# GpSimd's queue put under the kernel's own clock in a two-layer graph kernel

## The chip, the cores and the metric

The kernel runs as one program on one core of one Trainium2 chip. The metric is the device time of that core in microseconds, the median of three runs. The engines are named as the profile names them: PE (TensorE, with PEld for its weight loads), DVE (VectorE), ACT (ScalarE), POOL (GpSimd) and SP (SyncE, which here only issues transfers).

## The reference

Input is `x`, 64 batches of 256 x 256 in float32, and one adjacency `adj` of 256 x 256. Two layers follow each other, each with a layer norm and a ReLU ahead and a residual sum behind:

```python
# layer 0: three products with (adj * adj), two ReLUs between them
h = jnp.maximum(_layernorm(x, axis=-1), 0.0)
x = x + _L0_gnn_ref(h, adj, adj, L0_gnn_W1, L0_gnn_W2, L0_gnn_W3)
# layer 1: needs the eigenvectors U of the normalised Laplacian of adj
h = jnp.maximum(_layernorm(x, axis=-1), 0.0)
x = x + _L1_gnn_ref(h, adj, L1_gnn_W1, L1_gnn_b1, L1_gnn_W2, L1_gnn_b2)
#   _L1: _, U = jnp.linalg.eigh(L_norm); agg = U^T h; h = relu(agg W1 + b1); U (h W2 + b2)
```

Layer 0 does not need U. Layer 1 does, from its first product with U on.

## The kernel before

Two kinds of work run side by side on one core.

**The chain.** Class `Eigen` computes U step by step, mostly on DVE with operands of a few hundred columns: `laplacian`, `tridiagonalize` (254 Householder steps), `leaves` (32 QL steps on small blocks), and `level` four times (blocks of 32, 64, 128 and 256 are merged). PE serves it with small transposes and products into the banks `psA` to `psD`, ACT with squares and copies, POOL with column operations: powers (`power`, a `pow`), copies and masks.

**The layers.** Class `Layers` takes the 64 batches as 32 pairs. `products` is the stream of PE and ACT work of layer 0 (banks `bank`), `rows` the stream of norms. POOL has two kinds of work from them. A norm has three steps on POOL after eight reductions on ACT: `v` (scale and epsilon), `scale` (a `pow` on four columns), `shift`; ACT's ReLU waits for `shift`. And from pair 1 on each pair has three accumulating transfers issued from POOL's queue: `forms<-forms` in `spread_by_seven` and `s<-s` and `s<-forms` in `add`; products behind them wait for their landing.

**The order.** Class `Pace` sees every operation of the chain as it is written (`chain`) and keeps a clock of its own: for each engine the time up to which it is planned, for each tile when it was written and read. Before a chain operation is issued, `run(limit, engine)` issues what the streams have that can start before the chain's operation is due. `due` is when the operation's inputs are ready by that clock, plus 0.4 us for PE and 0.1 us for ACT; whether its engine is free by then isn't part of it. `fits` decides for one stream operation: for PE and ACT its whole length can count, for every other engine it needs only to start before the limit. `issue` advances the clock; for DVE and POOL it lets the clock lag behind an operation by up to `WINDOW` = 1.0 us.

This written order is binding only for the engines that `manual_schedule` names. Around the chain these are PE and ACT. The order of DVE, POOL and SP is left to the framework's scheduler, which lists the instructions anew by its own estimates. In layer 1 (`layer1`, with the last stream) all engines keep the written order. The conditional block `mend`, which is not taken, stands between them.

**A step of the tridiagonalisation, on POOL.** In the first 127 steps (`lo < P`) the written order of POOL's operations is, with the tiles' names of the profile: copy of `alpha` (`m<-xr`), masked column (`xc<-xc,lower`), `power(s0, ...)` (`s<-nn,half`), sign (`q<-xr`), and in the next turn of the loop `none` twice, `gg`, `gu`. DVE's `nb` (`m<-q,s`) needs `s` and `q`; `ac` needs `nb`; `den` needs `nb` and both `none`; `gam` (`z<-den`) needs `den`. The lines from the loop, which are shown shortened, give the order in which they are written:

```python
self.stt(nb, q, 2.0, s0, OP.mult, OP.mult)
self.stt(ac[:, hs], rc[:, hs], nb, xa[:, hs], OP.mult, OP.add)
pu, pr = as_row("psB", ac, halves), as_row("psA", rc, halves)   # PE transposes
nc.gpsimd.tensor_scalar(none, tail, 1e-30, 1e30, OP.is_le, OP.mult)
nc.gpsimd.tensor_tensor(none, none, nn, OP.add)
...
self.stt(den, alpha, nb, none, OP.mult, OP.add)
self.recip(gam, den)
...
aside(lo).tensor_tensor(gg, gam, gam, OP.mult)
```

In the other 127 steps POOL has only the copy, a memset of one column of `xc`, and both `none`. In `leaves` it has one copy a step (`zn`), in each `level` six powers of `rdq`, one of `zh` and one of `rn`.

Of the kernel before, what the change touches and what calls it, by code (L numbers as in the profile page):

```python
# [159 lines left out]
class Pace:  # L160
# [56 lines left out]
        return self.issue(op, self.slower)  # L217

    def fits(self, op, start, limit, engine):
        if engine is None or op.engine not in ("PE", "ACT"):  # L220
            return start < limit
        if engine == "PE":
            return start < limit + self.HOP * (op.engine == "ACT")
        return start + op.busy + self.lead * (op.engine == "ACT") < limit
# [2107 lines left out]
@with_exitstack  # L2332
def tile_kernel(ctx: ExitStack, tc: tile.TileContext, ap):
    pool = ctx.enter_context(tc.tile_pool(name="shared", bufs=1))
    gt2, u, ut = (pool.tile([P, H, N], F32, name=c) for c in ("gt2", "u", "ut"))
    layers = Layers(tc, ctx, ap, gt2, u, ut)
    layers.open(ctx)
    pace = Pace(tc.nc)
    with ExitStack() as inner:
        eigen = Eigen(tc, inner, ap, gt2, pace)  # L2340

        layers.nc = pace.later
        for op in layers.load(0):
            pace.chain(op)
        layers.nc = pace.now
        eigen.load_matrices(1, 2)
        layers.load_weights()
        eigen.load_rest()

        layers.nc, layers.now = pace.later, pace.now  # L2350
        pace.streams = layers.streams()
        with tc.manual_schedule(engines={mybir.EngineType.PE, mybir.EngineType.Activation}):
            eigen.vectors(u, ut)
            pace.go_on(FLAG_US)
        pace.on = False
        eigen.mend(u, ut)
    pace.on, pace.no_haste, pace.slower = True, True, 1.0
    layers.open1(ctx)
    layers.layer1(pace)
# [33 lines left out]
```

## Time and profile before

| | |
|---|---|
| time, median of 3 runs | 2365.49 us (2364.38 to 2368.03) |
| profiled execution | 2369.36 us, span 2367.6 us |
| mean granted clock of PE | 0.994 |
| PE busy, by stage: 0 to 40 us (start) | 22.79 of 40 us |
| 40 to 752 us (tridiagonalisation, first half) | 697.18 of 712 us |
| 752 to 1300 us (second half) | 538.67 of 548 us |
| 1300 to 1686 us (leaves) | 375.02 of 386 us |
| 1686 to 2178 us (levels) | 474.99 of 492 us |
| 2178 us to the end (layer 1) | 181.52 of 189.6 us |
| DVE busy in the five stages from 40 us on | 664.89, 520.75, 355.87, 368.04, 68.66 us |
| POOL busy in the same | 352.48, 151.30, 39.11, 62.16, 81.10 us |

Nearly every instruction is recorded by one helper line (208, the call in `Pace.issue`), so the profile's groups are told apart by tiles, not by lines. An entry "A <- B: 12.9, 32, 1.9" of the waits means that A sat idle 12.9 us in total in 32 places until B came, 1.9 us at the longest. In timeline rows the first number is the start, the second the duration, and the square bracket the idle time of the engine before it with what ended that.

### The profile page before, as it was taken

To read this page: it belongs to the slowest core of one execution; us is meant where nothing else is said; L and a number is where in the kernel's file an instruction comes from. 1 tells how busy PE (TensorE), PEld (TensorE's weight loads), DVE (VectorE), ACT (ScalarE), POOL (GpSimd) and SP (SyncE) were. 2 spreads that over 40 slices of the span, in tenths; PEclk is the share of its full clock that TensorE was granted. 3 is DMA by queue.
4 is the path that set the end of the run, shared out by engine and by line. 5 is a ranking of instruction groups with operands and counts; after the bars stand their busy time and mean duration, and the time that the engine had idled before them with its cause. 6 is when DMAs were issued, how large, how long until landed. Compare 5 with 4: busy or idle time off the path is not lost. (4 is left out here: it accounts for less than half of the span.)

```text
span 2367.6 us, 40804 instructions
## 1 busy us (share of the span) xinstructions
PE 2290.2 (97%) x10652; PEld 1854.7 (78%) x10652; DVE 2005.0 (85%) x12072; ACT 1183.8 (50%) x2951; POOL 698.7 (30%) x1946
## 2 busy tenths in 40 slices
PE   7999999999999999999999899999999999999999
PEld 4687878787777877787888788777778777887888
DVE  7999999999999999999999899999877687882343
ACT  4455554555555555555555345555554455543322
POOL 3444544445554222222222001111111111111443
PEclk9999999999999999999999999999999999999999
DMA  4022222122222222222222222322322222223675
GB/s 134 23 70 61 65 57 70 51 69 63 59 59 62 72 56 61 69 67 59 72 63 60 58 63 72 72 72 59 72 63 63 59 58 72 54 63 103 217 251 203
DMA packets 91359, 183.26 MB, mean 77 GB/s; under 512 B 8432, under 2 KB 61808, under 8 KB 91120
## 3 DMA queue, kind: packets, MB, share of 16 engines
q0 software_dynamic: 13392, 73.14, 15.6%
q1 hardware_dynamic: 77728, 107.45, 13.4%
q8 instruction: 86, 1.41, 0.2%
q14 instruction: 153, 1.25, 0.2%
HBM read 65.48 MB, written 41.94 MB: 45 GB/s over the span
## 5 line engine op out<-in xcount | busy, mean ns | idle before, releaser
L208 PE MATMUL bank<-forms,L_gnn_W 128*128 128x256 f32 (+2 forms) x2102 | 490.7, 382 | 9.2 <-DVE x L208 6.1
L208 PE MATMUL bank<-L_gnn_W,s 128*128 128x256 f32 x2086 | 476.0, 378 | 4.8 <-ACT s L208 4.7
L208 PEld LDWEIGHTS bank<-forms,L_gnn_W 128*128 128x128 f32 x2102 | 390.6, 191 | 73.3 <-issue 11.7
L208 PEld LDWEIGHTS bank<-L_gnn_W,s 128*128 128x128 f32 x2086 | 391.7, 192 | 57.3 <-ACT s L208 5.7
L208 ACT ACTIVATE s<-bank 128x512 f32<-128x512 f32 (+1 forms) x485 | 278.7, 579 | 174.3 <-PE bank L208 173.3
L208 PE MATMUL bank<-forms,sums 128*128 128x256 f32 (+1 forms) x1512 | 347.0, 377 | 0.0
L208 PEld LDWEIGHTS bank<-forms,sums 128*128 128x128 f32 x1512 | 283.3, 191 | 53.4 <-issue 15.5
L208 PE MATMUL bank<-gt,s 128*128 128x256 f32 (+1 forms) x1036 | 246.3, 377 | 1.1 <-ACT s L208 1.1
L208 PE MATMUL bank<-L_gnn_W,y 128*128 128x512 f32 (+3 forms) x538 | 230.8, 572 | 1.1 <-ACT y L208 1.1
L208 ACT ACTIVATE forms<-bank 128x512 f32<-128x512 f32 x217 | 128.9, 594 | 180.9 <-PE bank L208 180.7
L208 PEld LDWEIGHTS bank<-gt,s 128*128 128x128 f32 x1036 | 188.9, 190 | 24.8 <-ACT s L208 2.6
L208 POOL COPY m<-xr 128x1 f32<-128x1 f32 x254 | 59.9, 236 | 418.1 <-DVE xr L208 418.0
L208 PEld LDWEIGHTS bank<-L_gnn_W,y 128*128 128x128 f32 x538 | 98.7, 190 | 98.2 <-issue 87.3
L208 ACT ACTIVATE junk<-xr 128x254 f32<-128x254 f32 (+63 forms) x127 | 46.0, 362 | 200.5 <-DVE xr L208 200.4
L208 ACT ACTIVATE junk<-x 128x256 f32<-128x256 f32 x256 | 105.8, 413 | 71.9 <-issue 44.0
L208 DVE SCALAR_TENSOR_TENSOR A<-xr,wc,A 128x255 f32<-128x255 f32 (+63 forms) x381 | 139.2, 368 | 0.0
L208 DVE SCALAR_TENSOR_TENSOR A<-wr,q,A 128x255 f32<-128x255 f32 (+63 forms) x381 | 138.0, 365 | 0.0
L208 ACT ACTIVATE junk<-x,nm 128x256 f32<-128x256 f32 x256 | 128.7, 503 | 4.0
L208 PE MATMUL bank<-p,gt 128*128 128x512 f32 (+2 forms) x272 | 122.8, 567 | 0.0
L208 PE MATMUL bank<-gt,h 128*128 128x256 f32 (+1 forms) x520 | 119.1, 379 | 0.1
L208 DVE SCALAR_TENSOR_TENSOR r<-A,xr 128x255 f32<-128x255 f32 (+63 forms) x381 | 117.8, 309 | 0.2
L208 PE MATMUL psB<-ident,ac 128*128 128x128 f32 x381 | 84.7, 277 | 27.2 <-DVE z L208 15.0
(614 smaller groups left out, 4639.5 us busy)
## 6 DMA issues: line engine op xcount, KB each, us to landing
x<-in_x_dram SPq DMA_DIRECT2D x128, 256.0 KB, 3.0
x<-x SPq DMA_DIRECT2D x64, 512.0 KB, 3.5
forms<-forms POOLq DMA_DIRECT2D x31, 768.0 KB, 5.8
s<-s POOLq DMA_DIRECT2D x31, 768.0 KB, 5.9
s<-forms POOLq DMA_DIRECT2D x31, 768.0 KB, 5.8
hw<-hw SPq DMA_DIRECT2D x64, 256.0 KB, 3.1
out_dram<-out SPq DMA_DIRECT2D x64, 256.0 KB, 2.2
L_gnn_W<-in_L_gnn_W_dram SPq DMA_DIRECT2D x1, 2048.0 KB, 11.2
```

What stands on the lines that cost most here:

```text
L208: return op.call(*op.args, **op.kwargs)
```

## The change

POOL joins the engines whose written order is binding around the chain, and `fits` gets a rule for it: when the chain's next operation is one of POOL, a stream's operation for POOL goes ahead of it only if it would also end before the chain's is due. When the chain's next operation is one of another engine, a POOL operation of the streams still needs only to start before the limit. The order on PE and ACT stays written by the same clock, that of DVE and SP stays with the framework's scheduler. No instruction is added or taken away.

```diff
     def fits(self, op, start, limit, engine):
+        if engine == "POOL" == op.engine:
+            return start + op.busy < limit
         if engine is None or op.engine not in ("PE", "ACT"):
             return start < limit
...
-        with tc.manual_schedule(engines={mybir.EngineType.PE, mybir.EngineType.Activation}):
+        with tc.manual_schedule(engines={mybir.EngineType.PE, mybir.EngineType.Activation, mybir.EngineType.Pool}):
             eigen.vectors(u, ut)
             pace.go_on(FLAG_US)
```

## The prediction

> **What bounds the kernel now.** The busy times of the page come first.
>
> ```profile
> PE 2290.2 (97%) x10652; PEld 1854.7 (78%) x10652; DVE 2005.0 (85%) x12072; ACT 1183.8 (50%) x2951; POOL 698.7 (30%) x1946
> ```
>
> PE has 2290.2 us of work in a span of 2367.6 us. The change adds no work for it, so the time can only move by PE's idle time, now 77.4 us: 17.2 us before 40 us, 14.8 and 9.3 in the two halves of the tridiagonalisation, 11.0 in the leaves, 17.0 in the levels, 8.1 in layer 1 (from the busy times by stage). Second, the list of waits, all engines, for who holds PE and DVE up:
>
> ```profile
> DVE m L208 <- PE psB L208: 40.7, 4, 13.1
> ...
> DVE r L208 <- PE psB L208: 22.6, 75, 1.0
> ...
> PE psB L208 <- DVE z L208: 15.0, 19, 1.9
> DVE m L208 <- POOL s L208: 12.9, 32, 1.9
> ```
>
> The first row is the levels: the chain there waits for PE in four places, up to 13.1 us, so a POOL step that holds the chain up by a few us costs nothing. The second and third are the tridiagonalisation: in 75 steps the chain waits for PE, in 19 PE for the chain. There the two run neck and neck and a late chain costs PE time. The last is POOL's part: 32 times `nb` (m) waited for the power. Third, POOL's timeline in a usual step (its copy at 158.78 is left out) and in one of five steps that had the written order already:
>
> ```profile
> 158.93 0.51 POOL L208 TENSOR_SCALAR q<-xr 128x1 f32<-128x1 f32 x1
> 159.41 0.20 POOL L208 TENSOR_TENSOR xc<-xc,lower 128x2 f32<-128x2 f32 x1
> 159.70 0.32 POOL L208 TENSOR_SCALAR none<-m 128x1 f32<-128x1 f32 x1
> 160.10 0.61 POOL L208 TENSOR_TENSOR s<-nn,half 128x1 f32<-128x1 f32 x1
> 160.69 0.35 POOL L208 TENSOR_TENSOR none<-none,nn 128x1 f32<-128x1 f32 x1
> ```
>
> ```profile
> 472.74 0.29 POOL L208 TENSOR_TENSOR xc<-xc,lower 128x2 f32<-128x2 f32 x1
> 473.25 0.66 POOL L208 TENSOR_TENSOR s<-nn,half 128x1 f32<-128x1 f32 x1 [0.23 <-DVE nn L208]
> 473.91 0.26 POOL L208 TENSOR_SCALAR q<-xr 128x1 f32<-128x1 f32 x1
> 474.25 0.26 POOL L208 TENSOR_SCALAR none<-m 128x1 f32<-128x1 f32 x1
> 474.59 0.24 POOL L208 TENSOR_TENSOR none<-none,nn 128x1 f32<-128x1 f32 x1
> ```
>
> Now q and the first `none` go ahead of the power s; then s goes first and q and both `none` come behind it. Fourth, the largest idle stretch of PE in the levels: POOL's timeline, PE's, and the windows' row (columns: stretch, length, busy PE, PEld, DVE, ACT, POOL, granted clock, DMA share, GB/s).
>
> ```profile
> 1764.14 0.72 POOL L208 TENSOR_TENSOR rdq<-rdq,half 128x2 f32<-128x2 f32 x1 [4.36 <-DVE rdq L208]
> 1764.94 0.19 POOL L208 TENSOR_SCALAR v<-v 128x4 f32<-128x4 f32 x1
> 1765.22 1.01 POOL L208 TENSOR_TENSOR scale<-v,rsqrt 128x4 f32<-128x4 f32 x1
> 1766.30 0.20 POOL L208 TENSOR_TENSOR shift<-nm,scale 128x4 f32<-128x4 f32 x1
> ```
>
> ```profile
> 1769.61 2.93 PE L208 MATMUL bank<-L_gnn_W,s 128*128 128x256 f32 x6 [3.76 <-ACT s L208]
> ```
>
> ```profile
> 1768.50:1772.70 4.20, 3.09 (x7) 2.52 (x8) 0.18 (x1) 4.20 (x8) 0.00 (x0) 0.50 0.54 186
> ```
>
> A norm's steps stood behind the chain's power, which waited for DVE. ACT's last reduction for `v` ended at 1762.25. PE then sat 3.76 us and ran 4.2 us at half clock, 2.1 us more.
>
> **The change part by part.** All is set against the profiled span (2367.6 us; that execution took 2369.36) and carried to the median of 2365.49 as a difference.
>
> *1. Levels: the norm no longer stands behind the chain's power.* The chain is ahead of PE there (40.7 us of waits), so by the planner's clock, which goes with PE, the norm's steps come first. From 1762.3 they need 0.19 + 1.01 + 0.20 and some 0.15 of gaps, to 1763.85, before the power's input (DVE's rdq, ending 1763.98). ACT is free at 1763.89, so its ReLU, which started at 1766.54, comes 2.65 us earlier; 1.1 us of the gap stay. A gap of 2.47 us at 1326 kept full clock, so the half clock goes too: -2.65 - 2.1 = -4.7 us. Bounds: 0 (order unchanged) and -5.9. In the leaves and levels the other steps (zn, zh, rn, 0.2 to 0.7 us each) may now queue behind a norm or a transfer (0.97 us to issue); the cover is the 40.7 us, which if gone would make each such wait cost its 1 us.
>
> *2. First half: the power goes ahead.* Of the 12.9 us, six waits are followed at once by an idle PE (23.36, 492.71, 537.94, 559.37, 630.00, 678.78: 1.62, 0.95, 0.42, 0.96, 1.43, 0.66, in all 6.0 us). The `none` ahead of s takes about 0.32 to 0.40 us from its start to that of s (159.70 to 160.10); norms pushed ahead of the copy make up the rest. So between 6 x 0.32 = 1.9 and 6.0 us; I take -3.5, near the middle, as part of the norms stay in front.
>
> *3. First half: both `none` come later.* In the five steps of written order `den` waited 0.07, 0.07, 0.17, 0.02 and 0.13 us, 0.092 on average, so 127 x 0.092 = 11.7 us on the chain. PE pays only where it had no other work: in 48 of the 127 steps the transposes began within 0.2 us of the end of `ac`. 48 x 0.092 = +4.4 us. In one of the five (583 us) DVE had `ac` ahead of `den`; if the scheduler did that everywhere, PE's transposes would come 0.13 us earlier, -2.3 us in the 18 recorded waits; with queued durations at their means `none` is 0.16 us late, +7.7. Bounds -2.3 and +7.7.
>
> The row that speaks against this part is the sign step: q takes 223 to 723 ns, 458 in the middle, for one column. [...]
>
> *4. Layer steps ahead of `none`.* This is the price that no row shows. In the program `none` is written behind `ac` and PE's transposes, and before a PE operation the streams may put on POOL whatever starts up to 0.4 us after `ac` is ready; the new rule guards only POOL's own operations. The scheduler had `none` ready before `den` in all but 12 steps. I took the time at which each layer step got its input from ACT, and counted those from 0.35 us before the end of `nn` to 0.46 us after `ac`: 26 of 50 in the first half, 20 of 40 in the second. With 1.0 us for a transfer, 1.25 for a norm's first two steps and 0.6 for the two `none`, `den` is late by 39.4 and 24.6 us, 64 in all, 1.39 a step. Behind it wait z, gc and gr on DVE, and with them the next step's transposes. Of each 1.39 us, 0.82 fit into the median time from `ac` to DVE's read of the transposes, and 0.25 into the mean slack of PE (0.40 less the least, 0.15): 0.32 x 46 = 14.7 us. A third of it I take as planned for already, since the chain's 22.6 us of waits for PE are room that the planner left and the chain didn't use: +10 us. Bounds 0 (all hidden) and 64 - 22.6 = 41.
>
> The rest goes together: the memset of `xc` in the second half now stands between the copy and `none` (0.12 us, beside DVE's work), and the DMAs issued are the same, on the same queue; SP's are not moved.
>
> Sum: -4.7 - 3.5 + 4.4 + 10 = +6.2, so 2371.7 us.
>
> **The rivals.**
>
> *Faster.* The scheduler lists DVE with POOL's new order in view and puts `ac` and the read of the transposes ahead of a late `den`; then parts 3 and 4 cost nothing, and 1 and 2 stay: 2365.5 - 8.2 = 2357.3. For it: the order of 583 us was of that kind. It decides if `den` is late by less than the 0.82 us hole in most of the 46 steps. Against: DVE is busy 664.9 of 712 us there, so displaced work finds little room.
>
> *No change.* Part 4 is half hidden and half planned, +2 in place of 10: 2363.7.
>
> *Much slower.* The chain outgrows its cover. After 2178 us PE has only 58 matmuls of layer 0 left beside layer 1: 42 of 0.215 us, 8 of 0.43, 8 of 0.11, 13.4 us. If half of the 64 us stays on the chain, with 11.7 from part 3 and less 3.5, it is 40 us longer; past 13.4 every us counts: +27 - 4.7 = 2388.
>
> **How the numbers follow.** The forecast gets 0.38, much slower 0.12, no change 0.22, faster 0.28. Three runs of before lie within 0.15%, so about 0.2% (4.7 us) is what can be told from no change. Chances: faster 0.28, same 0.22, slower 0.50. The range reaches from 2355 (the faster case and its bound in part 1) to 2389; the forecast's own is 2364 to 2382.
>
> **What would show it.** Right: the idle time at 1769 falls to about 1 us without a half clock; `m <- POOL s` falls below 5 us; `den <- POOL none`, 3.6 us now, rises above 20; norms and transfers stand between q and `none`; PE's waits for the chain before 1300 us rise from 27 to 35 us or more. Wrong: `den <- POOL none` stays under 10 us, or PE's idle time falls below 70 us.

## The result, and the profile after

| | before | after |
|---|---|---|
| median | 2366.35 us (2364.38 to 2368.03, 4 runs) | 2396.16 us (2394.48 to 2398.02, 4 runs) |
| ratio | | 1.0126, 95% interval 1.0109 to 1.0144 |
| profiled execution | 2369.36 us, span 2367.6 | 2394.48 us, span 2392.7 |
| PE idle, 40 to 752 and 752 to 1300 us | 14.8 and 9.3 us | 32.2 and 21.4 us |

The kernel is 29.8 us slower. The two profiled executions lie 25.1 us apart, since that of before is 3.0 us above its median and that of after 1.7 us below. PE has the same instructions; of the 25.1 us, 22.5 are more idle time of PE (99.9 in place of 77.4 us) and 2.6 more busy time:

```profile
PE 2292.8 (96%) x10652; PEld 1852.9 (77%) x10652; DVE 2011.9 (84%) x12072; ACT 1180.6 (49%) x2951; POOL 688.6 (29%) x1946
```

The list of waits of all engines shows who made PE and DVE idle:

```profile
DVE rb L208 <- POOL rdq L208: 46.5, 24, 6.7
...
DVE den L208 <- POOL none L208: 39.3, 53, 2.3
...
PE psB L208 <- DVE z L208: 29.0, 29, 2.5
...
DVE r L208 <- PE psB L208: 26.5, 57, 2.0
...
PE psB L208 <- DVE xr L208: 23.0, 30, 2.3
```

`den` waits 39.3 us for `none`, where it waited 3.6. The profile puts PE's waits for its transposes down to `z` (29.0 us, before 15.0), which comes from `den`, and to the next row `xr` (23.0, before 10.6). The transposes themselves read `ac`, not `z`; all waits put down to `z` lie in steps in which DVE has `den` ahead of `ac`. Both rows tell that the chain comes late for PE. The first row is the levels' part, and harmless, as will be seen.

PE's order is the same in both kernels, all 10652 matmuls in the same sequence (ACT's too, but for one copy at 43 us). So the start of each matmul after, less its start before, is a lag that can be followed (times are those of before):

| at | 90 us | 302 | 460 | 775 | 1093 | 1357 | 1700 | 1754 | 1932 | 2162 | 2277 |
|---|---|---|---|---|---|---|---|---|---|---|---|
| lag, us | -2.3 | 11.7 | 16.2 | 22.6 | 30.8 | 38.5 | 41.6 | 41.4 | 29.8 | 27.7 | 25.0 |

Up to 1357 us, early in the leaves, the lag grows by 40.8 us, in the rest of the leaves by 3.1; the levels give 13.9 back, layer 1 another 2.7. This last part goes with the clock: behind PE's stops at 2158 and 2194 us, of 4.8 and 2.8 us in both kernels, the half clock lasted 6.8 us each before and 3.4 us each after. The -2.3 us at 90 us are no effect of the change: a kernel whose POOL is left to the scheduler until 1300 us shows -1.8 there, and the profiled execution of before lies 3.0 us above its median.

A bad step, with the second longest wait of all, by POOL's timeline of after and by DVE's:

```profile
195.67 0.36 POOL L208 TENSOR_SCALAR q<-xr 128x1 f32<-128x1 f32 x1
197.30 0.19 POOL L208 TENSOR_SCALAR v<-v 128x4 f32<-128x4 f32 x1 [1.27 <-ACT junk L208]
197.58 1.03 POOL L208 TENSOR_TENSOR scale<-v,rsqrt 128x4 f32<-128x4 f32 x1
198.68 0.24 POOL L208 TENSOR_SCALAR none<-m 128x1 f32<-128x1 f32 x1
199.00 0.19 POOL L208 TENSOR_TENSOR none<-none,nn 128x1 f32<-128x1 f32 x1
```

```profile
196.81 0.22 DVE L208 SCALAR_TENSOR_TENSOR ac<-A,m,xa 128x2 f32<-128x2 f32 x1
...
199.23 0.22 DVE L208 SCALAR_TENSOR_TENSOR den<-m,none 128x1 f32<-128x1 f32 x1 [2.13 <-POOL none L208]
...
200.14 0.38 DVE L208 SCALAR_TENSOR_TENSOR r<-psB,xr 128x229 f32<-128x229 f32 x1
```

After the sign step POOL has the norm's `v` next. Its input isn't there: POOL stands for 1.27 us with both `none` ready behind it, then does `v` and `scale`. `den` waited 2.13 us. DVE had done `ac` before that, and PE began the transposes at 198.16, but their read (`r<-psB`) stands behind `den` on DVE and comes late with it. In 47 places with a layer step ahead of `none`, `den` waited over 0.15 us, 38.2 us in all; up to 21.7 us of this fall into the time in which POOL stood idle for the layer step's input.

How much of the lag that explains: between the ends of successive `nn`, the step lengths of both kernels can be subtracted. 67 of the 249 steps compared have a layer step ahead of the second `none`; they grew by 24.4 us (34 steps, first half) and 17.3 us (33, second half), 41.7 in all. The 182 others changed by +1.1 and -4.3 us.

In the levels, the place that the prediction had chosen, by POOL's timeline, PE's, and the windows' row of after:

```profile
1803.72 0.23 POOL L208 TENSOR_SCALAR v<-v 128x4 f32<-128x4 f32 x1 [4.09 <-ACT junk L208]
1804.04 1.01 POOL L208 TENSOR_TENSOR scale<-v,rsqrt 128x4 f32<-128x4 f32 x1
1805.02 0.69 POOL L208 TENSOR_TENSOR rdq<-rdq,half 128x2 f32<-128x2 f32 x1
1805.68 0.20 POOL L208 TENSOR_TENSOR shift<-nm,scale 128x4 f32<-128x4 f32 x1
```

```profile
1808.99 3.29 PE L208 MATMUL bank<-L_gnn_W,s 128*128 128x256 f32 x14 [1.75 <-ACT s L208]
```

```profile
1808.00:1812.20 4.20, 3.21 (x15) 2.86 (x16) 3.05 (x24) 4.20 (x7) 0.69 (x1) 1.00 0.39 125
```

The norm no longer stands behind the power, though the power slipped in between `scale` and `shift`. PE's stop fell from 3.76 to 1.75 us, and the clock stayed full. And a second stop went that the prediction hadn't touched, here PE's timeline of before and of after at the same matmul:

```profile
1878.49 2.07 PE L208 MATMUL bank<-forms,L_gnn_W 128*128 128x256 f32 x4 [3.61 <-DVE x L208]
```

```profile
1908.33 3.62 PE L208 MATMUL bank<-forms,L_gnn_W 128*128 128x256 f32 x16
```

Before, a layer's addition on DVE (`x<-x,bank`) came late because DVE was deep in the chain's work. The chain's lead explains it, by the waits between 1725 and 2205 us of after:

```profile
DVE m L208 <- PE psB L208: 7.0, 4, 3.5
```

It was 40.7 us. POOL's `rdq` now stands behind layer steps, DVE waits 46.5 us for it in place of 20.7, and so the chain no longer runs ahead of PE. That the addition finds room in these waits is read from the two traces; no run took the one without the other.

### The profile page after: what moved, and what is told of

It reads as the page before. It is cut to its first block, busy times and chain, and to the rows that moved or that the text cites. A ratio compares the mean times of both kernels' runs of the same rounds, so it can differ in the third digit from the quotient of the medians.

```text
span 2392.7 us, 40790 instructions
## 1 busy us (share of the span) xinstructions
PE 2292.8 (96%) x10652; PEld 1852.9 (77%) x10652; DVE 2011.9 (84%) x12072; ACT 1180.6 (49%) x2951; POOL 688.6 (29%) x1946
## 3 DMA queue, kind: packets, MB, share of 16 engines
q1 hardware_dynamic: 77728, 107.45, 13.5%
## 5 line engine op out<-in xcount | busy, mean ns | idle before, releaser
L208 PEld LDWEIGHTS bank<-forms,L_gnn_W 128*128 128x128 f32 x2102 | 390.5, 191 | 69.1 <-issue 11.7
L208 PEld LDWEIGHTS psB<-ident,ac 128*128 128x128 f32 x381 | 45.8, 136 | 116.7 <-issue 61.1
```

What stands on the lines that cost most here:

```text
L208: return op.call(*op.args, **op.kwargs)
```

## The experiments

Each is set against the kernel before on the same chip.

| kernel | median | before | ratio, 95% |
|---|---|---|---|
| `none` first, planner's order redrawn | 2369.54 | 2367.28 | 1.0013 (1.0003 to 1.0022) |
| bound from the leaves on | 2357.72 | 2367.28 | 0.9960 (0.9946 to 0.9974) |
| bound in the tridiagonalisation only | 2404.06 | 2367.28 | 1.0161 (1.0144 to 1.0178) |
| without the rule in `fits` | 2397.84 | 2367.28 | 1.0131 (1.0114 to 1.0148) |
| `none` first, PE's order kept | 2359.69 | 2367.62 | 0.9967 (0.9954 to 0.9979) |
| the same, with a load on POOL | 2413.68 | 2367.62 | 1.0188 (1.0171 to 1.0205) |
| the same, old order of the chain's steps | 2357.08 | 2367.62 | 0.9954 (0.9938 to 0.9971) |
| a wider rule | 2426.01 | 2367.62 | 1.0236 (1.0219 to 1.0254) |
| bound from the levels on | 2353.69 | 2367.03 | 0.9945 (0.9931 to 0.9958) |

**1. `none` first, planner's order redrawn.**

```diff
             nb = nbs[:, k : k + 1]
+            none = self.col("none", 1)
+            nc.gpsimd.tensor_scalar(none, tail, 1e-30, 1e30, OP.is_le, OP.mult)
+            nc.gpsimd.tensor_tensor(none, none, nn, OP.add)
...
             pu, pr = as_row("psB", ac, halves), as_row("psA", rc, halves)
-            (the same three lines)
```

> POOL's order is still written out for the whole kernel; only the two instructions that make `none` are written at the top of the step, ahead of `ac` and of PE's transposes, so that no layer step can be put between q and them. Theory 1 (the time went into layer steps that stand ahead of `none`: 67 steps, 41.7 us, with 13.5 us given back in the levels): about 2350 to 2360 us, and `den <- POOL none` falls from 39.3 us to below 8. Theory 2 (the chain order s, q, none itself is slower, as such): 2385 to 2400 us, with `den <- POOL none` about as now.

2369.54 us. 27 us of the loss went with two instructions that were written some lines earlier, and `den` waits 5.3 us. 22 steps keep a layer step ahead of `none` (it stands ahead of the copy or the sign step there); they grew by 0.03 us in all, so a layer step costs nothing there, and its place is what counts. But the time lies 10 us above theory 1's range, which left out that the planner's clock, which now counts `none` earlier, draws PE's order anew (10688 matmuls in place of 10652, as the planner cuts some in two).

**2, 3. One part of the kernel at a time.** `vectors` is split behind the tridiagonalisation; only the blocks for which POOL is named differ.

```diff
         with tc.manual_schedule(engines={PE, Activation}):
-            eigen.vectors(u, ut)
+            reflections = eigen.vectors(u, ut)      # tridiagonalisation
+        with tc.manual_schedule(engines={PE, Activation, Pool}):
+            eigen.behind(u, ut, reflections)        # leaves, levels
```

> POOL's order is written out from the leaves on only; in the tridiagonalisation the scheduler orders POOL as in the kernel before. Theory 1 (the loss is in the tridiagonalisation, the gain of 13.5 us in the levels is independent of it): 2350 to 2355 us, the stop of PE near 1769 us short and at full clock, PE's idle time before 1300 us as in the kernel before. Theory 2 (the levels give time back only because the tridiagonalisation ran late and left less to catch up): 2362 to 2368 us, no gain.

> POOL's order is written out in the tridiagonalisation only; from the leaves on the scheduler orders POOL. Theory 1 (both parts are independent): 2396 + 13.5 = about 2410 us (2404 to 2412). Theory 2 (the levels' recovery comes with the late start, not with POOL's order): 2393 to 2399 us.

2357.72 and 2404.06 us (in the third kernel Pool is named in the first block and not in the second). Against before on the same chip that is -9.6 and +36.8, together +27.2; the change as a whole brought +29.8. So the two parts are independent to within 2.6 us, and theory 2 falls in both. Run 2 is 3 us above theory 1's range, run 3 at the lower end of its own, 6 us under its number. For run 2 the same lags show why: that kernel loses 5.2 us in the leaves (from -0.6 at 1250 us to +4.6 at 1700), before the levels give 13.5 back. Run 9 takes that up. For run 3, the leaves' loss, which it doesn't have, makes up 4 of the 6 us.

**4. The rule in `fits` left out.**

```diff
-        if engine == "POOL" == op.engine:
-            return start + op.busy < limit
```

> All of the change but the new rule in `fits`: a chain operation of POOL is then fitted into the clock with PE's 0.4 us of grace, like the others. PE's and ACT's order stay the same, POOL's differs in some hundred places. Theory 1 (the rule guards POOL's own operations only, and the loss comes in front of PE's operations, which it doesn't guard): within 0.5% of the change, 2392 to 2408 us, `den <- POOL none` 39 us or somewhat more. Theory 2 (the rule itself is what makes the order bad, by pushing layer steps from q and s to the place behind them): 2365 to 2380 us, `den <- POOL none` well below 39 and `m <- POOL s` back at 10 or more.

2397.84 us, `den` waits 39.1 us for `none`. (PE's 0.4 us of grace, which the expectation names, don't enter for a POOL operation: without the rule a layer's step needs only to start before the chain's is due.) The rule made no difference that can be told: it guards the places in front of POOL's own operations, and the costly ones lie in front of PE's transposes.

**5. `none` first, with PE's order kept.** The planner's clock still counts `none` at its old place; only the instructions are written earlier.

```diff
             nb = nbs[:, k : k + 1]
+            none = ...    # both instructions, written directly, not by the clock
...
-            nc.gpsimd.tensor_scalar(none, ...)
-            nc.gpsimd.tensor_tensor(none, ...)
+            self.planned(...)    # the same two: counted by the clock, not written
```

> As the kernel with `none` at the top of the step, but the planner's clock still counts the two `none` at their old place, so that PE's and ACT's orders stay those of the change, matmul for matmul; only POOL's order differs, with 27 layer steps left ahead of `none` (all of them ahead of the copy or the sign step too) in place of 69. Theory 1 (layer steps ahead of `none` are the whole loss, and the 15 us that the first experiment lacked were PE's redrawn order): 2396.2 - 41.7 = 2354.5 us (2350 to 2359). Theory 2 (those 15 us belong to POOL's written order): 2365 to 2372 us.

2359.69 us, all 10652 matmuls in the order of the change. So 36.5 us of the change's time are the place of `none` behind the layer steps, and 9.9 us of the first experiment's time came with PE's redrawn order. The time lies 0.7 us above theory 1's range and 5.2 above its number; `den` still waits 7.5 us here, which theory 1 had left out, but no run separates that. The wait:

```profile
DVE den L208 <- POOL none L522: 7.5, 24, 0.6
```

**6. A load of known size at the disputed place.**

```diff
+            if k < 120 and k % 2 == 0:
+                spare = self.sp.tile([P, 4], F32, tag="spare", name="spare")
+                gpsimd.tensor_tensor(spare, ones[:, 0:4], ones[:, 4:8], OP.pow)
             none = ...
```

> The same kernel with one more POOL instruction, a power of 128x4 on a scratch tile (1.03 us in the norms), between q and the first `none` in every second one of the first 120 steps: 60 in all. It measures what a layer step at this place costs. A transfer there (1.05 us with its gap) made `den` wait 0.5 us. Theory 1 (every wait of `den` goes through to the end, nothing hides it): 60 x 0.5 to 0.6 = +30 to +36 us against the kernel without the load, `den <- POOL none` about 30 us more. Theory 2 (0.82 us on DVE and 0.25 us of PE's slack hide it, as predicted): within 5 us of the kernel without the load.

2413.68 us, 54.0 us more than run 5. The waits:

```profile
DVE den L208 <- POOL none L525: 74.2, 80, 1.2
...
PE psB L208 <- DVE z L208: 58.2, 65, 2.1
```

`den` waits 66.7 us more than in run 5: 1.11 us for each of 60 loads, about the load and its gap; `none` had no slack to speak of. Theory 1 had taken half of it from the transfers and was too low. Of 66.7 us, 54.0 came through to the end, 0.90 us a load or 81%. So a wait of known size, put there by hand, goes four fifths of the way through: the hiding that the prediction relied on, 1.07 us a step, would have taken nearly all of it.

**7. The chain's POOL steps in the scheduler's old order**, on top of run 5: q, `none`, s, `none` in `length`.

```diff
             if lo < P:
+                gpsimd.tensor_scalar(q, ...); gpsimd.tensor_scalar(none, ...)
                 self.power(s0, nn, 0.5)
+                gpsimd.tensor_tensor(none, none, nn, OP.add)
-                nc.gpsimd.tensor_scalar(q, ...)
```

> As the kernel whose `none` is moved without a change of PE's order, but in the first half the chain's four POOL steps stand as the scheduler had them: q, the first `none`, the power s, the second `none`. Theory 1 (parts 2 and 3 are small, and about cancel): within 4 us of that kernel, with `m <- POOL s` back at 5 to 13 us. Theory 2 (the power ahead of q and `none` is what gains, 3.5 us as predicted or up to 6, and later `none` costs nothing): 4 to 8 us slower than that kernel. Theory 3 (later `none` costs 4.4 us and more): 3 to 6 us faster.

2357.08 us, 2.6 us faster than run 5, within theory 1's 4 us; the lag at 775 us is -0.4 us against +2.3 in run 5, so it is the first half. The waits:

```profile
DVE m L208 <- POOL s L208: 13.4, 37, 1.2
```

This wait of `nb` for the power is back, a little above the 5 to 13 us of theory 1, and the kernel is still not slower. In run 5 it is absent, but `nb` waits 5.2 us for q there, which comes behind the power.

**8. A wider rule.**

```diff
-        if engine == "POOL" == op.engine:
-            return start + op.busy < limit
+        if op.engine == "POOL" and engine is not None:
+            return start + op.busy < limit - self.LATER.get(engine, 0.0)
```

> The change with its rule in `fits` made wider: a layer's POOL step goes ahead of a chain operation of any engine only if it ends before that operation is ready, PE's 0.4 us and ACT's 0.1 us of grace taken off. PE's order is drawn anew by this; 50 steps keep a layer step ahead of `none` in place of 69, since PE's transposes are ready only after the place where `none` is due. Theory 1 (the loss goes by the number of such steps and their lateness): 2396 - (19 x 0.62 = 12) = 2384 us, 2375 to 2390. Theory 2 (steps that end in time by the clock do no harm): 2355 to 2370 us.

2426.01 us: slower than the change, against both theories. `den` waits less, 20.6 us, as meant; but PE gets through fewer matmuls, 3142 and 2441 in the two stretches in place of 3221 and 2515 with the change, by the windows of this kernel (PE is the first pair of numbers):

```profile
40.00:752.00 712.00, 669.81 (x3142) 530.39 (x3141) 646.79 (x3211) 356.87 (x951) 333.09 (x1033) 0.99 0.23 56
752.00:1300.00 548.00, 512.55 (x2441) 414.07 (x2441) 515.86 (x4007) 279.65 (x699) 146.21 (x593) 0.99 0.25 60
```

PE is idle for 42.2 and 35.5 us, with the change 32.2 and 21.4, and its mean granted clock there is 0.99, with the change 1.00. `run` looks only at the head of a stream, so a POOL step that the rule turns away also holds back the matmuls behind it. That this is the cause of the idle time is argued from the code and from PE's idle time, not shown by a run of its own.

**9. Bound from the levels on.** As run 2, split behind the leaves.

> POOL's order is written out from the levels on only; in the tridiagonalisation and the leaves the scheduler orders POOL as in the kernel before. In the kernel bound from the leaves on, the same matmuls ran 0.6 us early at 1250 us of the kernel before, but 4.6 us late at 1700 us, and 8.9 us early behind the levels. Theory 1 (the leaves lose about 5 us by their written order, on their own): 2357.7 - 5 = about 2353 us, 2350 to 2355. Theory 2 (the 5 us in the leaves are only moved, the levels would have lost or waited for them): 2356 to 2359 us, as the kernel bound from the leaves on.

2353.69 us, 0.55% faster than the kernel before, and the best of the study. The lag is +0.9 us at 1700 us and -12.6 behind the levels. So the leaves' 4.0 us are a loss of their own, and the gain in the levels stands alone.

The four effects, from pairs of medians: levels -13.3 (run 9 against before), leaves +4.0 (run 2 against 9), the chain's own order +2.6 (run 5 against 7), layer steps ahead of `none` +36.5 (the change against run 5). Their sum is +29.8, the change's measured +29.8. That it closes to the tenth is luck: the pairs leave out that run 7 and run 2, which the sum takes as equal, are 0.6 us apart, and the kernel before, run anew beside each group, has medians from 2366.35 to 2367.62 us.

## Why the prediction was wrong

The direction was right, the size was not: +6.2 us forecast, +29.8 measured, above the range's end. The step that failed is part 4, **"layer steps ahead of `none`"**: +10 taken, bounds 0 to 41, measured +36.5. Within it, what was mis-sized most is the hiding of the late `none`: DVE's hole, PE's slack and the room in the plan.

- *The mechanism and the count held, the lateness nearly.* 46 late steps were counted from ACT's times, and 47 waited: 26 and 21 in the two halves, against 26 and 20 (that they are the same steps isn't shown). Taken from the end of the `r<-A` ahead of it, `den` starts 72.8 us later than before in the 67 steps with a layer step, against 64 forecast. Its waits are only 38.2 us, since DVE does other steps in the meantime: `ac` ahead of `den` in 26 of the 34 such steps of the first half, in 12 of them the read of the transposes too.
- *The hiding on DVE was somewhat too large.* The prediction let it take 37.7 of 64 us (46 x 0.82). The 67 steps grew by 41.7 us in all, so some 31 of the 72.8 us were hidden on DVE. That "0.82 fit into the median time from `ac` to DVE's read of the transposes" took a stretch of time for a hole. DVE's timeline of before, in a usual step, shows what is in it:

```profile
161.35 0.21 DVE L208 SCALAR_TENSOR_TENSOR den<-m,none 128x1 f32<-128x1 f32 x1
161.49 0.21 DVE L208 SCALAR_TENSOR_TENSOR ac<-A,m,xa 128x2 f32<-128x2 f32 x1
...
161.69 0.15 DVE L208 RECIPROCAL z<-den 128x1 f32<-128x1 f32 x1
...
161.88 0.26 DVE L208 TENSOR_SCALAR gc<-ac,z 128x2 f32<-128x2 f32 x1
...
162.59 0.40 DVE L208 SCALAR_TENSOR_TENSOR r<-psB,xr 128x234 f32<-128x234 f32 x1 [0.19 <-PE psB L208]
```

The stretch holds `z`, `gc` and what follows from `den`, which move with it. DVE's idle time before that read was 0.15 us on average in the first half and 0.06 in the second. Cover was only this and the steps that don't need `den`. Both could have been seen in the trace of before.

- *The room behind DVE was not there.* Of what was left on the chain, the prediction took 11.5 us (46 x 0.25) as hidden by PE's slack, and a third of the rest as "planned for already", together 16 us. Measured, 36.5 of the chain's 41.7 us reached the end, so this took about 5. It is the largest part of the miss of 26.5 us: some 11.1 come from here, 8.8 from the lateness and 6.6 from DVE. In run 6, where DVE keeps `den` ahead of `ac` in 121 of the first 127 steps (before 125), 81% of the waits passed; the prediction let 16% of the lateness pass (10 of 64), and 50% did.
- With 36.5 in place of 10, and the rest of the prediction's sum left as it was, the time would have been 2398. That the sum missed by 23.6 and not 26.5 us is luck: the levels gave more than forecast. The upper bound of 41 held, but by luck too: it takes 22.6 us of room off 64, and the lateness was larger and the room smaller. The range didn't use this bound, which makes 2403 by the prediction's sum, and ended behind the slowest rival, at 2389.

The other steps. *Part 1* was right at its place: the lag fell by 4.8 us there (41.4 to 36.6) against 4.7 forecast, but by two errors that cancel. The stop fell by 2.0 us in place of 2.65 (the power of 0.69 us stands between `scale` and `shift`), and the half clock had lasted longer than the 4.2 us that were looked at, by the windows' row of before:

```profile
1768.50:1775.30 6.80, 5.69 (x13) 4.54 (x14) 0.18 (x1) 4.49 (x8) 0.00 (x0) 0.50 0.33 116
```

5.69 us of work at half clock are 2.8 us lost, not 2.1: the 16 matmuls behind the stop took 6.55 us before and 3.72 after, at full clock. What part 1 missed is the second stop, 3.61 us and again 6.7 us at half clock with 6.11 us of work (3.1 us; before, the first 8 matmuls behind it took 3.78 us, after, the same row has 16 in 3.62). The two stops make 11.5 of the levels' 13.3 us. The leaves' "cover of 40.7 us" is the levels' and does not hold for them: +4.0. *Parts 2 and 3* were forecast at -3.5 and +4.4, +0.9 together; together they measured +2.6. Part 2 overlooked that q moves behind the power and that `nb` needs both. Part 3's 0.092 us per step is what run 5 shows too: 10.4 us of waits in 114 clear steps of the first half (clear: without a layer step ahead of `none`).

The row that the prediction set against part 3, the sign step of 223 to 723 ns, did not decide: the 89 clear steps of the first half after, in the order s, q, `none`, `none`, grew by 1.1 us in all, 0.01 a step. POOL's steps and DVE's updates of A overlap in time: in the step shown of before POOL's power (160.10 to 160.71) ran beside the updates that began at 159.84 and 160.53 and took 0.45 and 0.46 us, and no such update (`A<-wr,q,A`, `A<-xr,wc,A`) took over 0.48 us in either trace.

The rivals: *no change* needed more room behind DVE, where there was less. *Faster* saw right that DVE would put `ac`, and at times the read, ahead of a late `den`; but by its own sign `den` had to be late by less than 0.82 us in most steps, and it was late by more in 44 of the 67. *Much slower* came closest in time but not in kind: PE lost its time within the tridiagonalisation and did not run out of work at the end. Of the signs, one missed: the stop at 1769 us kept 1.75 us, not about 1. PE's waits for the chain in the tridiagonalisation, told as 35 us or more in place of 27, came to 56.3 (`z`, `xr` and `ac`).

## What to carry to other kernels

When an order by a planner's clock is made binding for an engine that stands for a step without its input while ready ones wait behind it (POOL here, 1.27 us in the step shown), look for every short step of the critical chain that is written later than it is ready: whatever the planner puts ahead of it can cost its own duration (1.11 us a load in run 6) and the wait for its own input. Before calling a late operation hidden, list the instructions in the hiding stretch and strike out all that depend on it; only the idle time and the steps that don't need it are cover. Ask of each further allowance (slack of another engine, room in the plan) where the trace shows it. And bind an engine stage by stage: the same order was worth -13.3 us in one stage and +36.5 in another.

## What the runs showed of the hardware

A stop of PE of the same length at the same matmul did or didn't bring the half clock. PE's timeline of before and of after, and the windows' row behind the latter:

```profile
1326.29 0.46 PE L208 MATMUL psD<-bs,mask 128*128 128x128 f32 x2 [2.47 <-DVE rb L208]
```

```profile
1363.46 0.46 PE L208 MATMUL psD<-bs,mask 128*128 128x128 f32 x2 [2.47 <-DVE rb L208]
```

```profile
1364.60:1367.90 3.30, 3.30 (x11) 2.77 (x11) 2.36 (x16) 0.97 (x2) 0.00 (x0) 0.50 0.01 2
```

Before, the clock stayed full behind it (1.00 from 1326 to 1330 us); after, it was halved. In run 9 it was slower too: the six `bank` matmuls from 1326.66 us took 2.73 us, where run 3's, behind the same stop, took 1.46. In run 3, at the matmul of 1769.61 us, even the stop of 3.76 us kept the full clock (1.00 from 1804 to 1816 us there). From 40 us on, no stop under 2.38 us halved it in the traces of before and after; the one of 2.38 us did, at 137.93 us of after, and the one of 2.46 us at 153.46 us did not. A half clock inside the span lasted 6.8 us in each of four places before, and 3.4 us in each of four after.

So stops of 2.47 and of 3.76 us went either way, and the length alone did not decide; what did is not shown, as no run moved a stop on purpose. The half clock's share of the levels' gain, some 3 us for each of two stops in the execution that was profiled, may thus be partly chance there. Not all of it is: the mean granted clock of all executions was 0.993 to 0.997 in the nine of before that stand beside run 9, and 0.998 in each of run 9's five. The prediction's evidence for full clock, one stop of 2.47 us, was thinner than it looked.
